# Linear attention after an AMM convolution block: heads re-sorted over row groups, two products of eight tiles for four of four, fewer matmuls in the averages, new ranks

## The chip, the cores and the metric

The kernel runs on one core of one Trainium2 chip. The metric is the device time of one execution in microseconds, lower is better. Engines are named as in the profile: PE (TensorE matmul), PEld (TensorE weight load), DVE (VectorE), ACT (ScalarE), POOL (GpSimd), SP (SyncE, which issues the DMAs).

## The reference

The input is x of 32 images, 1024 channels, 14 x 14 positions, float32. Layer 0 (table look-up convolutions with softmax weights, three of them, with batch norms) ends in a residual sum. Layer 1 is what the change is about; cut to what matters:

```python
x = gn(x)                                   # 32 groups of channels per image
q = elu(qk_w[:c] @ x[:, :half] + b) + 1     # 1024 channels out of 512
k = elu(qk_w[c:] @ x[:, half:] + b) + 1
q_rope, k_rope = rope(q), rope(k)           # pairs of channels turned by an angle of the position
# 16 heads of 64 channels, n = 196 positions
z   = 1 / (einsum('bhdn,bhd->bhn', q, k.mean(-1)) + 1e-6)
kv  = einsum('bhdn,bhen->bhde', k_rope, x) / n
out = einsum('bhdn,bhde->bhne', q_rope, kv) * z
x = x + out + depthwise_3x3(x) + lepe_b     # "lepe": nine taps per channel
```

The last einsum, `q_rope` times `kv`, is the query product.

## The kernel before

Layer 0 is written as three stages one after the other and fills the span to about 2277 us. Layer 1 follows under one instruction plan for 16 pairs of images (NP = 16).

**The plan.** `Plan.do(engine, rank, weight, fn, reads, writes, port, lag)` records a piece: a few instructions on one engine, with a rank (its due time) and a weight (an assumed duration). `Plan.write()` plays the pieces through: an engine that is free takes the ready piece of lowest rank whose buffers are free. The order so found is the order of each engine's instructions; on the chip they run in that order and wait on semaphores. `due` holds the ranks within a pair, `T` the step of ranks from pair to pair. Buffers are `Slot`s out of rings; PSUM has eight banks, in three rings: `mm` (4), `pa` (3) and `w` (1).

**One pair.** Channels lie in eight blocks of 128 partitions; `xts[h]` holds four of them (h = 0 or 1).
- `front` (8 pieces per pair): ACT scales a block into a `w` bank (L1639), DVE adds the third convolution's output (L1648), applies the ReLU and the residual (L1653) and takes statistics (L1658).
- `group_norm` (twice): PE averages the statistics over the 32 partitions of a group with the matrix `gavg`; two halves of each image are two matmuls that accumulate (L1695), once for the means and once for the variances, with small DVE steps between (L1703 to L1711).
- `channels` (16): the projection to q or k, 128 output channels by 392 positions, four matmuls (L1786), then two ACT pieces (L1795, L1798) and one on DVE (L1802). The even channels of a rope pair lie in r = 0, the odd ones in r = 1, so a q tile holds four heads, 32 partitions each, in two halves r.
- `rope` (8): four POOL instructions per tile. `v_tokens`, `k_tokens` (16): PE transposes, copied out by ACT (L1848, L1851). `products` (4): kv of four heads, eight or more small matmuls each in 32-column tiles (L1885).
- `normalisers`: DVE writes the means of k into `kmm` (L1918, two pieces), PE multiplies (L1936), DVE adds 1e-6 (L1945) and takes the reciprocal (L1946); the result goes through DRAM and back as a broadcast, and POOL multiplies it into the q tile (L1972).
- `attend` (4 pieces, one per q tile j): 16 matmuls in the code, 32 in the profile, since each float32 matmul shows as two (L1992). Head h of the tile contracts over partitions 32h to 32h+31 and writes 64 output channels: the tile on the array has 32 rows and 64 columns. Heads 0 and 1 write the two halves of one `pa` bank, heads 2 and 3 those of another, so the four tiles of a piece take each row group once.
- `lepe` (8): the eight side taps are added by DVE onto the `pa` bank (L2010), but one tap of each of blocks 4 to 7, which ACT and POOL do (`side_tap`, L2039 and L2047); then DVE adds the bank to x (L2024), which frees it. The middle tap is folded into the residual by ACT (L1752).
- The last pair has no successor to overlap with; there six of its eight blocks have their taps done on PE with diagonal matrices (`diagonal_taps`, L2066) before the query product accumulates onto them.

**Inputs.** Small tables and the first pair's x are loaded by SP during the third convolution: that stage calls one entry of the list `early` at the start of each of its 13 groups. The projection weights take the place of the convolution's tables, so `projection` issues their eight loads (L230) when layer 1 begins.

Of the kernel before, what the change touches and what calls it, by code (L numbers as in the profile page):

```python
# [17 lines left out]
P = 128  # L18
C = 1024
# [130 lines left out]
def conv_preact_kernel(ctx: ExitStack, tc: tile.TileContext, a: dict, out: bass.AP):  # L150
# [274 lines left out]

    def attention_inputs(stack):
# [3 lines left out]
        def loads(_):  # L430
# [6 lines left out]
            for n, k in (("qb", a["qb"]), ("kb", a["kb"].rearrange("o (r j p) -> p (o r) j", p=P, r=2))):  # L437
                nc.sync.dma_start(tile_(n, [P, 2, 4]), k)
                tile_(n + "u", [P, 2, 4])
                tile_(n + "d", [P, 2, 4])  # L440
# [3 lines left out]
            for n in ("cosq", "sinq"):  # L444
                t = tile_(n, [P, 4, 14])
                v = a[n].rearrange("p j (r c) -> p j r c", c=14)
                nc.sync.dma_start(t[:, :2], v[:, :2, :, 0])
                nc.sync.dma_start(t[:, 2:], v[:, 2:, 0, :])
# [12 lines left out]
            for h in (1, 0):  # L461
                for i in range(2):
                    nc.sync.dma_start(
                        given[f"x{h}"][:, :, i * HW : (i + 1) * HW],
                        x[i, 4 * h * P : 4 * (h + 1) * P].rearrange("(c q) n -> q c n", q=P),
                    )

# [28 lines left out]
        def projection(b):  # L496
            t = a["wkT" if b < 4 else "wqT"]
            return lambda: load_lut(b, t[(b % 4) * P : (b % 4 + 1) * P])

        return [loads, third, tables, heads], [projection(b) for b in range(8)], [third]  # L500
# [990 lines left out]
    with ExitStack() as s:  # L1491
# [57 lines left out]
        T = 80.0  # L1549
# [22 lines left out]
        for n, k in (("mm", 4), ("pa", 3), ("w", 1)):  # L1572
# [8 lines left out]
        for n, shape in (  # L1581
# [3 lines left out]
            ("gq", [P, 8, 2]),  # L1585
            ("gve", [P, 8]),
# [41 lines left out]
        def front(p, h, c, xt, ot, rank):  # L1628

            ch = 4 * h + c  # L1630
            w = Slot("pa" if p == 0 and c % 2 else "w")
# [49 lines left out]
        def group_norm(p, h, rank):  # L1681
# [10 lines left out]
            def average(ps, src):  # L1692
                def piece():
                    for k in range(2):
                        nc.tensor.matmul(  # L1695
                            ps()[:, :8], gavg, src[:, :, k], start=(k == 0), stop=(k == 1)
                        )

                return piece

            def centred():
# [5 lines left out]
                )  # L1707
                nc.vector.tensor_scalar(g("nmc"), pm()[:, :8], -1.0, None, ALU.mult)
# [18 lines left out]
            do(PE, rank, 0.42, average(pm, mean), gst, [pm], lag=0.3)  # L1727
            do(DVE, rank, 0.55, centred, [pm, *gst], [key("gq"), key("nmc")])
            do(PE, rank, 0.42, average(pv, g("gq")), [key("gq")], [pv], lag=0.3)
# [45 lines left out]
        def channels(p, keys, j, r, t, sums, rank):  # L1775
# [7 lines left out]
            def product():  # L1783
                m0 = r * 512 + j * P
# [87 lines left out]
        def products(i, jp, kts, vts, rank):  # L1872
# [4 lines left out]
            def piece():  # L1877
                pv = pk()[:, :256].rearrange("p (j r e) -> p j r e", j=2, r=2)
                for j in range(2):
                    for r in range(2):  # L1880
                        for h in range(2):
                            for q in range(4):
                                c0 = (2 * (2 * jp + j)) * P + 64 * q
# [29 lines left out]
        def normalisers(p, qs, ks, rank):  # L1913


            def means(i):
                def piece():
                    nc.vector.tensor_tensor(  # L1918
# [9 lines left out]
            for i in range(2):  # L1928
                do(DVE, rank - 10, 0.2, means(i), allk, [("kmm", i)], port=True)
# [14 lines left out]
            def inverse():  # L1944
                nc.vector.tensor_scalar(z, pd()[:, :HW], 1e-6, None, ALU.add)  # L1945
                nc.vector.reciprocal(z, z)  # L1946
# [6 lines left out]
            do(DVE, rank - 10, 1.7, inverse, [pd], ["z"])  # L1953
# [27 lines left out]
        def attend(j, kvs, qr, pa, rank, onto):  # L1981

            def piece():
                for i in range(2):
                    for r in range(2):
                        for h in range(4):
                            v = slice(32 * h, 32 * h + 32)
                            n = 210 - 14 * i  # L1990
                            e = slice(64 * (h % 2), 64 * (h % 2) + 64)
                            nc.tensor.matmul(  # L1992
                                pa[h // 2]()[e, i * 210 : i * 210 + n],
                                kvs[i, j // 2]()[v, j % 2, r],
                                qr()[v, r, i * HW : i * HW + n],
                                start=(r == 0 and not onto),
                                stop=(r == 1 and (i == 1 or not onto)),
                            )

            do(PE, rank, 1.65, piece, [kvs[0, j // 2], kvs[1, j // 2], qr], pa, lag=0.25)  # L2000
# [76 lines left out]
        def store(p, h, xt, rank):  # L2077
# [14 lines left out]
        unread = once.tile([P, HW], F32, tag="unread", name="unread")  # L2092


        due = dict(
            front_k=-64,
            front_q=-30,
            channel=9.0,
            norm=19,
            normalised=33,  # L2100
            middle=43,
            key=7.75,
            rope_k=-1.5,
            query=23,
            step=7.25,
            row=4.25,
            rope_q=74,
            v0=27,
            v_half=1.75,
            v1=69,  # L2110
            k0=41,
            k_half=3.0,
            k1=64,
            kv0=65,
            kv1=55,
            den=45,
            scaled=70,
            attend=75.5,
            sums=24,
            lepe=98,  # L2120
            taps=9.0,
            half=16.0,
            tap=2.75,
            side=99,
            diagonal=160,
        )

        def pair(p, t):
# [46 lines left out]
            js = (2, 3, 0, 1)  # L2175
            for n, j in enumerate(js):
                normalise_q(p, n, j, qrs[j], at["scaled"])
            last = p == NP - 1
            pools = {0: "pa pa", 1: "mm mm", 2: "pa w", 3: "mm mm"} if last else {}
# [99 lines left out]
```

## Time and profile before

| | |
|---|---|
| median of 3 runs | 3359.23 us (3357.97 to 3359.8) |
| profiled execution, its own time | 3358.99 us |
| its span | 3357.2 us |
| first projection of layer 1 (PE L1786) | at 2295.4 us |
| last query product (PE L1992) | at 3348.6 us |
| PE / DVE / POOL / ACT busy over the span | 98% / 85% / 75% / 53% |
| granted PE clock of the core | 0.994 |

A "busy" PE is not a PE at its peak: matmuls overlap. Here PE is read by the start of one piece to the start of the next, and an engine's load by the busy time within a stretch of whole pairs.

### The profile page before, as it was taken

How to read it: one execution, taken by the hardware profiler on the slowest of the kernel's cores; microseconds unless marked ns; L12 is line 12 of the kernel's file. 1: busy time of each engine (PE TensorE's matmuls, PEld its weight loads, DVE VectorE, ACT ScalarE, POOL GpSimd, SP SyncE). 2: the span in 40 equal slices, each digit the busy share in tenths (PEclk: the TensorE clock that was granted, in tenths of full speed). 3: DMA queues.
4: the chain of work that ended last, by engine and by line, in shares of the span. 5: the costliest groups of instructions: out<-in, count | busy, mean ns of one | idle time of the engine just before them, and what ended most of it. 6: DMA issues, size and time to landing. Idle time of an engine off the chain costs nothing. (4 is left out here: it accounts for less than half of the span.)

```text
span 3357.2 us, 61041 instructions
## 1 busy us (share of the span) xinstructions
PE 3296.6 (98%) x22297; PEld 2014.2 (60%) x22297; DVE 2864.6 (85%) x4174; ACT 1787.8 (53%) x4419; POOL 2534.2 (75%) x1558
## 2 busy tenths in 40 slices
PE   8999999999999999999999999998999999999999
PEld 4555555554454544444478888885666666666665
DVE  8999999997888899888656666755899999999996
ACT  5555555554444444444311111107888888888886
POOL 6999999997788889888432222215988888888888
PEclk9999999999999999999999999999999999999999
DMA  4110111103444344433231111113223333232321
GB/s 120 47 49 28 46 47 35 39 28 86 135 124 123 112 122 125 122 113 109 64 81 50 50 50 50 39 47 125 70 84 99 90 89 98 79 92 82 94 81 49
DMA packets 242251, 266.31 MB, mean 79 GB/s; under 512 B 32812, under 2 KB 239700, under 8 KB 241944
## 3 DMA queue, kind: packets, MB, share of 16 engines
q1 hardware_dynamic: 241248, 262.02, 26.3%
q8 instruction: 179, 2.93, 0.4%
q14 instruction: 128, 1.05, 0.1%
q10 hardware_dynamic: 696, 0.31, 0.0%
HBM read 171.01 MB, written 75.58 MB: 73 GB/s over the span
## 5 line engine op out<-in xcount | busy, mean ns | idle before, releaser
L622 POOL TENSOR_TENSOR t<-t,r 128x1568 f32<-128x1568 f32 (+3 forms) x288 | 961.8, 3340 | 519.7 <-issue 221.2
L742 PE MATMUL po<-t,lut 128*128 128x392 f32 x3840 | 1331.2, 499 | 4.9 <-DMA t<-spare 3.9
L742 PEld LDWEIGHTS po<-t,lut 128*128 128x128 f32 x3840 | 710.1, 190 | 604.2 <-issue 79.4
L1786 PE MATMUL mm<-y,lut 128*128 128x392 f32 x2048 | 714.5, 494 | 1.4 <-DVE k L1802 1.4
L584 DVE STREAM_TRANSPOSE tt<-t 128x1568 f32<-128x1568 f32 (+1 forms) x284 | 517.4, 1822 | 153.9 <-ACT t L572 149.6
L572 ACT ACTIVATE t<-sc,cbias 128x392 f32<-128x392 f32 (+1 forms) x624 | 322.5, 598 | 558.5 <-PE sc L905 187.7
L2010 DVE SCALAR_TENSOR_TENSOR pa<-y,lepe_w,pa 128x406 f32<-128x406 f32 x900 | 535.7, 636 | 19.1 <-PE pa L1992 16.8
L615 DVE STREAM_TRANSPOSE r<-rc 128x1568 f32<-128x1568 f32 (+1 forms) x284 | 520.8, 1834 | 11.6 <-POOL t L622 1.2
L1786 PEld LDWEIGHTS mm<-y,lut 128*128 128x128 f32 x2048 | 369.4, 188 | 242.9 <-issue 6.3
L587 POOL TENSOR_TENSOR tt<-tt 128x784 f32<-128x784 f32 x256 | 471.0, 1840 | 30.3 <-DVE tt L584 30.3
L572 ACT ACTIVATE t<-sc,room 128x392 f32<-128x392 f32 x512 | 259.1, 589 | 392.7 <-issue 163.8
L1368 PE MATMUL po<-t,lut 128*128 128x224 f32 (+2 forms) x1352 | 313.3, 414 | 0.0
L603 DVE TENSOR_REDUCE sm<-tt 128x98 f32<-128x784 f32 (+1 forms) x284 | 293.6, 1034 | 1.1 <-POOL tt L587 0.8
L1368 PEld LDWEIGHTS po<-t,lut 128*128 128x128 f32 (+1 forms) x1352 | 233.4, 189 | 62.9 <-issue 60.6
L605 DVE RECIPROCAL rc<-sm 128x98 f32<-128x98 f32 (+1 forms) x284 | 220.1, 775 | 9.8
L626 ACT ACTIVATE sm<-sm 128x98 f32<-128x98 f32 (+1 forms) x284 | 85.4, 301 | 153.8 <-DVE rc L605 153.8
L1972 POOL TENSOR_TENSOR qr<-qr,zb 128x784 f32<-128x784 f32 x64 | 118.3, 1856 | 46.0 <-DMA zb<-zd 45.7
L1639 ACT ACTIVATE w<-x,tb,gn_a 128x196 f32<-128x196 f32 x248 | 128.3, 517 | 35.3 <-POOL y L1521 28.2
L1798 ACT ACTIVATE e<-e 128x392 f32<-128x392 f32 x256 | 134.4, 525 | 1.0
L1035 PE MATMUL sc<-patch,room 27*32 27x392 f32 x4096 | 122.9, 507 | 8.9 <-DMA patch<-h1d 8.9
L1381 DVE TENSOR_TENSOR o<-po,o 128x224 f32<-128x224 f32 (+1 forms) x156 | 81.5, 543 | 56.8 <-PE po L1368 51.9
L1752 ACT ACTIVATE y<-x,gb,ga 128x196 f32<-128x196 f32 x256 | 123.3, 541 | 12.1 <-POOL gb L1715 12.1
(215 smaller groups left out, 4517.9 us busy)
## 6 DMA issues: line engine op xcount, KB each, us to landing
patch<-h1d SPq DMA_DIRECT2D x383, 108.5 KB
x<-in_x_dram SPq DMA_DIRECT2D x32, 784.0 KB
o3d<-o SPq DMA_DIRECT2D x56, 448.0 KB
x<-in_x_dram SPq DMA_DIRECT2D x64, 392.0 KB
out_dram<-x SPq DMA_DIRECT2D x64, 392.0 KB
o<-o3d SPq DMA_DIRECT2D x62, 392.0 KB
h1d<-pad SPq DMA_DIRECT2D x96, 225.0 KB
patch<-h1d SPq DMA_DIRECT2D x383, 54.2 KB
```

The costliest lines, as they stand in the source:

```text
L572: nc.scalar.activation(t[:, j, : sc.shape[1]], sc, AF.Identity if exact else AF.Exp, bias=bias[:, j : j + 1],)
L584: nc.vector.transpose(tt, tf)
L587: nc.gpsimd.tensor_tensor(tv[:, :, :8], tv[:, :, :8], tv[:, :, 8:], ALU.add)
L603: nc.vector.tensor_reduce(sm, tv, AX.X, ALU.add)
L605: nc.vector.reciprocal(rc, sm)
L615: nc.vector.transpose(r, bc(rc, 2, KC))
L622: nc.gpsimd.tensor_tensor(v[:, c], v[:, c], r[:, c], ALU.mult)
L742: nc.tensor.matmul(po[h], luts[b][:, j, h * P : (h + 1) * P], ts[u % len(ts)][:, j, :N2], start=(b == 0 and j == j0), stop=(b == 7 and j = ...
L1368: nc.tensor.matmul(dst, w, x, start=start, stop=stop)
L1786: nc.tensor.matmul(pv(), w[kt][:, m0 : m0 + P], ywin(p, first + kt), start=(kt == 0), stop=(kt == 3),)
L1798: nc.scalar.activation(e(), e(), AF.Exp, scale=-1.0)
L2010: nc.vector.scalar_tensor_tensor(acc, neighbours(p, c, offset(k)), lw[:, c, k : k + 1], acc, ALU.mult, ALU.add,)
```

## The change

1. **Heads.** The projections' output channels are re-sorted, so that q tiles 2jp and 2jp+1 hold the heads (0, 3, 4, 7) and (1, 2, 5, 6) of the half jp, 32 partitions each. Row group q of the two tiles then holds the two heads of channel block c = q, one per column half. `attend` does both tiles in one piece: 32 matmuls in the code, in the order that goes over all eight 32 x 64 tiles, into four `pa` banks at once. There are two such pieces per pair, each with weight `ATT` = 2.0 where four had 1.65.
2. **Loads for it.** The weights are loaded by three DMAs of 32- and 64-element runs for each of the eight row blocks, in place of one DMA of whole rows; the biases and the angle tables, by 16 DMAs each, in four further entries of `early`.
3. **Averages.** DVE adds the two halves (`halves`, twice per `group_norm`), and each average is one matmul.
4. **Normalisers.** The two pieces for `kmm` go from DVE to POOL; adding 1e-6 goes from DVE to ACT, with the constant in a new tile `tiny`.
5. **Banks.** `mm` 4 and `pa` 4; `front` takes its bank from `mm`.
6. **Side taps** for blocks 0, 3, 4 and 7 in place of 4 to 7; in the last pair the first half's banks are `pa`, the second half's `mm`.
7. **Ranks.** All of `due`, and `T`.

```diff
+    HEADS_OF = (0, 3, 4, 7), (1, 2, 5, 6)
+    heads_in = lambda t: slice(1, 3) if t else slice(0, 4, 3)
...
+        def bias(n, k):
+            def piece(_):
+                for j in range(4):
+                    for o in range(2):
+                        for r in range(2):
+                            src = k[:, r, j // 2 * 2 + o].rearrange("(h d) -> h d", d=32)
+                            dst = given[n][64 * o : 64 * o + 64, r, j : j + 1]
+                            nc.sync.dma_start(dst, src[heads_in(j % 2)])
...
+        def angles(n):
+            def piece(_):
+                v = a[n].rearrange("(h d) j (r c) -> h d j r c", c=14, d=32)
+                for j in range(4):
+                    for q in range(4):
+                        o, h = divmod(HEADS_OF[j % 2][q], 4)
...
+                        nc.sync.dma_start(given[n][32 * q : 32 * q + 32, j], src)
...
-            return lambda: load_lut(b, t[(b % 4) * P : (b % 4 + 1) * P])
...
+            def load():
+                v = w[:, 32:480].rearrange("p (n m) -> p n m", m=64)
+                src = t[:, 64:960].rearrange("p (n m) -> p n m", m=P)
+                nc.sync.dma_start(v, src[:, :, 32:96])
+                nc.sync.dma_start(ends(w, 512), ends(t, C))
+                v = w[:, 512:].rearrange("p (n m) -> p n m", m=64)
+                nc.sync.dma_start(v, t.rearrange("p (n m) -> p n m", m=P)[:, :, 32:96])
...
-        return [loads, third, tables, heads], [projection(b) for b in range(8)], [third]
+        return [loads, qb, kb, angles("cosq"), angles("sinq"), third, tables, heads], [projection(b) for b in range(8)], [third]
...
-        T = 80.0
+        T = 81.22
+        SIDES = [0, 3, 4, 7]
+        ATT = 2.0
...
-        for n, k in (("mm", 4), ("pa", 3), ("w", 1)):
+        for n, k in (("mm", 4), ("pa", 4)):
...
-            w = Slot("pa" if p == 0 and c % 2 else "w")
+            w = Slot("pa" if p == 0 and c % 2 else "mm")
...
-                    for k in range(2):
-                        nc.tensor.matmul(
-                            ps()[:, :8], gavg, src[:, :, k], start=(k == 0), stop=(k == 1)
-                        )
...
+            def average(ps):
+                return lambda: nc.tensor.matmul(ps()[:, :8], gavg, g("gs"), start=True, stop=True)
+
+            def halves(src):
+                nc.vector.tensor_reduce(g("gs"), src, AX.X, ALU.add)
...
-            do(PE, rank, 0.42, average(pm, mean), gst, [pm], lag=0.3)
-            do(DVE, rank, 0.55, centred, [pm, *gst], [key("gq"), key("nmc")])
-            do(PE, rank, 0.42, average(pv, g("gq")), [key("gq")], [pv], lag=0.3)
+            do(DVE, rank, 0.1, lambda: halves(mean), gst, [key("gs")])
+            do(PE, rank, 0.21, average(pm), [key("gs")], [pm], lag=0.3)
+            do(DVE, rank, 0.65, centred, [pm, *gst], [key("gs"), key("nmc")])
+            do(PE, rank, 0.21, average(pv), [key("gs")], [pv], lag=0.3)
...
-                m0 = r * 512 + j * P
+                m0 = j % 2 * 512 + (2 * r + j // 2) * P
...
-                                c0 = (2 * (2 * jp + j)) * P + 64 * q
+                                c0 = 512 * jp + 64 * HEADS_OF[j][q]
...
-                    nc.vector.tensor_tensor(
+                    nc.gpsimd.tensor_tensor(
                         kmm[i].rearrange("p r j h -> p (r j) h")[:, :, i:8:2],
...
-                do(DVE, rank - 10, 0.2, means(i), allk, [("kmm", i)], port=True)
+                do(POOL, rank - 10, 0.3, means(i), allk, [("kmm", i)], port=True)
...
-                nc.vector.tensor_scalar(z, pd()[:, :HW], 1e-6, None, ALU.add)
-                nc.vector.reciprocal(z, z)
+            def more():
+                nc.scalar.activation(z, pd()[:, :HW], AF.Identity, bias=tiny)
...
-            do(DVE, rank - 10, 1.7, inverse, [pd], ["z"])
+            do(ACT, rank - 10, 0.3, more, [pd], ["z"])
+            do(DVE, rank - 10, 1.3, lambda: nc.vector.reciprocal(z, z), [], ["z"])
...
-        def attend(j, kvs, qr, pa, rank, onto):
+        def attend(jp, kvs, qrs, pas, rank, onto):
...
                     for r in range(2):
-                        for h in range(4):
-                            v = slice(32 * h, 32 * h + 32)
...
+                        for q in range(4):
+                            v = slice(32 * q, 32 * q + 32)
+                            for j in range(2):
+                                c, h = divmod(HEADS_OF[j][q], 2)
+                                nc.tensor.matmul(
+                                    pas[c]()[64 * h : 64 * h + 64, i * 210 : i * 210 + n],
+                                    kvs[i, jp]()[v, j, r],
+                                    qrs[j]()[v, r, i * HW : i * HW + n],
...
-            do(PE, rank, 1.65, piece, [kvs[0, j // 2], kvs[1, j // 2], qr], pa, lag=0.25)
+            do(PE, rank, ATT, piece, [kvs[0, jp], kvs[1, jp], *qrs], pas, lag=0.25)
...
-            front_k=-64,
-            front_q=-30,
-            channel=9.0,
...
-            attend=75.5,
-            sums=24,
-            lepe=98,
+            front_k=-58.62,
+            front_q=-30.11,
+            channel=17.14,
...
+            attend=93.22,
+            sums=8.99,
+            lepe=102.05,
...
-            pools = {0: "pa pa", 1: "mm mm", 2: "pa w", 3: "mm mm"} if last else {}
-            for n, j in enumerate(js):
-                pa = [Slot(b) for b in pools.get(n, "pa pa").split()]
-                by_pe = last and n < 3
+            for m, jp in enumerate((1, 0)):
+                pools = ["mm"] * 4 if last and m else ["pa"] * 4
+                pas = [Slot(b) for b in pools]
                 taps = {}
...
+                by_pe = [last and 2 * m + k // 2 < 3 for k in range(4)]
...
-                    for m in range(3 if last else c // 4):
+                    for _ in range(3 if last else c in SIDES):
...
+                attend(jp, kvs, qj, pas, at["attend"] + due["sums"] * 2 * m, by_pe)
```

## The prediction

> **What bounds the kernel now.** I read the busy times by stage first. Only layer 1 (2277 us to the end) is touched beyond a few loads, and it is periodic, so I took the chain of work that ended last and looked for the same step in successive pairs:
>
> ```profile
> 2932.58 2.64 PE mm L1786 x8
> 2997.00 2.64 PE mm L1786 x8
> 3061.72 2.68 PE mm L1786 x8
> 3126.17 2.71 PE mm L1786 x8
> 3190.80 2.64 PE mm L1786 x8
> ```
>
> The columns are start, length and step. A pair takes (3190.80 - 2932.58) / 4 = 64.55 us, and the chain stays almost wholly on PE. The busy times of just these four pairs (the columns are PE, PEld, DVE, ACT, POOL, then clock, DMA share and GB/s):
>
> ```profile
> 2932.60:3190.80 258.20, 256.18 (x2497) 166.63 (x2497) 248.41 (x528) 220.03 (x545) 228.52 (x208) 1.00 0.31 90
> ```
>
> Divided by four, PE has work in 64.05 of 64.55 us, DVE 62.1, POOL 57.1, ACT 55.0. PE sets the pace, but DVE has only 2.45 us per pair to spare. So whatever PE saves beyond that is worth nothing unless DVE is relieved too. The waits of DVE in these four pairs say what the 2.45 us consist of:
>
> ```profile
> DVE pa L2010 <- PE pa L1992: 3.5, 2, 1.9
> DVE q L1802 <- ACT e L1798: 1.8, 3, 0.9
> DVE w L1648 <- ACT w L1639: 1.5, 3, 0.8
> ```
>
> In total, number, longest: few and short. The costs of the PE pieces come from the timeline (start, length, then x instructions); the length of a piece includes the tail of its last matmul, so I take start to next start:
>
> ```profile
> 868.18 0.94 PE L1035 MATMUL sc<-patch,room 27*32 27x392 f32 x32
> 869.63 5.50 PE L742 MATMUL po<-t,lut 128*128 128x392 f32 x16 [0.51 <-DMA t<-spare]
> ...
> 2923.83 1.99 PE L1885 MATMUL mm<-vt,kt 105*32 105x64 f32 x128
> 2925.75 0.68 PE L1848 MATMUL mm<-ident,kr 128*105 128x128 f32 x4
> ...
> 2946.28 0.51 PE L1695 MATMUL mm<-gq,gavg 128*128 128x8 f32 x4
> 2946.72 1.60 PE L1992 MATMUL pa<-qr,kv 32*64 32x210 f32 x32
> 2948.25 2.90 PE L1786 MATMUL mm<-y,lut 128*128 128x392 f32 x8
> ```
>
> A query product takes 2948.25 - 2946.72 = 1.53 us for 32 matmuls, 48 ns each; an average 0.44 us (others 0.36 to 0.43).
>
> **Query products, per pair.** Now 4 x 1.53 = 6.1 us. A full-array matmul of 392 columns takes 2.64 / 8 = 0.33 us, so one of 203 (the mean of 210 and 196) streams for 0.17 us; 32 of them four at a time are 8 x 0.17 = 1.37 us, and the measured 1.53 is that and a start-up. So four tiles do run at once. Eight at a time would take 64 / 8 x 0.17 + 0.16 = 1.53 us for two q tiles: the lower bound. The upper one is no more overlap than now, 3.06 us. That more than four tiles overlap, columns of one row group included, is in the L1035 row: 32 matmuls of 392 columns in 32 x 32 tiles last 0.94 us in all, where eight in a row take 2.64. I take 1.9 us: the change books 2.0 in the plan, and the plan's weights stand 0.11 to 0.13 above the trace (1.65 for 1.53; 1.6 for the 1.47 of L1936; 1.15 for the 1.04 of 64 matmuls of L1885). Saved: 6.1 - 3.8 = 2.3 us (0 to 3.1). The piece after a product is late by 0.1 (2.74 for 2.64 us in L1786); two fewer of these, 0.2.
>
> The issue rate could stand in the way: 64 matmuls in 1.9 us are 30 ns each. L1885 shows 128 with their weight loads in 2925.75 - 2923.83 = 1.92 us, 15 ns each, so the row leaves room. The Trainium skill ("TensorE: Matmul & The Clock Gate", section "Wait — 56ns, not 53.3ns?") says that matmuls never start less than about 25 ns apart; by that floor the product would take 1.6 us, and the L1885 row is below the floor.
>
> **Averages.** Four pieces of about 0.41 us lose half of their matmuls: 4 x 0.2 = 0.8 us saved on PE. DVE gains four small reductions of 0.16 us (the nearest rows, L1708 and L1711, are 8 columns wide and last 0.156 and 0.158): +0.64 us (0.3 to 0.9, as they follow a dependent step or not). The second one lies between gq and the PE average, on the chain of the group norm, whose successor (POOL's power, then ACT's normalisation) has tens of microseconds of rank ahead of the projections: no cost but DVE's time.
>
> **Normalisers.** DVE loses two pieces of 0.39 us (L1918) and one of 0.35 (L1945): -1.13 us. POOL gains two of 128x32, between its own 0.2 us for 128x8 and DVE's 0.39: +0.6, to 57.7. ACT gains one of 196 columns, 0.36 as in L1806: to 55.4. Neither becomes the bound. What queues behind them are POOL's rope steps and ACT's exponentials; the ranks are ten before the due time, so that the wait for the reciprocal is not the last one.
>
> **Sum per pair.** PE 64.55 - 2.3 - 0.2 - 0.8 = 61.25; DVE 62.1 + 0.64 - 1.13 = 61.6. So DVE becomes the pace, by a hair, with PE next. Before, PE as the single bound lost 0.5 us of 64.55; two engines this near to each other lose more. If DVE keeps none of its 2.45 us of waiting the pair takes 61.6, if it keeps all 64.05. I take a third, the share that is hand-over from ACT (the lines L1798 and L1648 above and smaller ones, about 0.9 us per pair): 62.4 us. Gain 2.15 us per pair, for 15 steps from pair to pair 32 us.
>
> **Banks.** A product now needs all four `pa` banks empty, so DVE has no taps to do from its last sum onto x until the product is done; it has to fill some 2 to 5 us (1.9 for the product, and up to 2.64 for the projection that PE is in) from its 25 us per pair that are not taps or sums (62.1 less 60 x 0.55 and 8 x 0.47). That is cover enough if such work is ready; I price it at nothing here and as a rival below. `front` now shares `mm`: eight holdings of some 2.5 us beside 16 of about 5 for the projections and smaller ones, by my count under 60% of four banks.
>
> **The start.** Layer 1's first projection begins at 2295.4 and needs all four key weights. They were issued at 2277.7, behind two 392 KB loads:
>
> ```profile
> 2277.71 1.88 SPq L230 DMA_DIRECT2D lut<-in_wkT_dram  x4
> 2279.63 3.15 SPq L230 DMA_DIRECT2D lut<-in_wqT_dram  x4
> ...
> 2295.44 21.32 PE L1786 MATMUL mm<-y,lut 128*128 128x392 f32 x64
> ```
>
> At the 361 GB/s of that stretch 0.8 + 2.1 MB are there by about 2286. Now four weights are 4 x 128 x 17 = 8704 runs of 128 or 256 B. The old angle tables give the price of a short run: between 1703.2 and 1709.4 us there were
>
> ```profile
> DMA packets 8107, 0.26 MB, mean 42 GB/s; under 512 B 7891, under 2 KB 8107, under 8 KB 8107
> ```
>
> 8107 packets in 6.2 us on 16 engines, 12.2 ns each. 8704 such are 6.6 us, with the bytes' own 5.8 us on top 12.5: landing by 2293, just in time. The far bound is the mean packet of the stretch from 2277.5 (5163 packets in some 22.3 us on 16 engines: 69 ns, mostly bytes), which would make it 38 us and the start 24 us late. I take +1, the short-run row being the nearest in size. SP issues 24 DMAs for 8, at 0.47 to 0.79 us 8 to 13 us more; the loads behind them (x of pair 1, read by ACT at 2312) have 12 us or more to spare. The Trainium skill ("DMA: Bandwidth & Descriptors", section "Specifications") puts the least transfer for full rate at 512 B, which speaks against these runs; it gives no time for them.
>
> The 64 small loads of `early` go out 16 to a group, 0.43 to 0.7 us each: 7 to 11 us of SP, in a gap that SP has in each group (it issues at 1744.1 to 1746.0 and next at 1763.9): hidden. Without the gap they would delay the t<-t transfers by as much, four times.
>
> **The tail.** The last pair's final product now holds all four blocks of the first half, two of which have five DVE taps each to come; before, those two were attended at 3328.4 and their taps ran under PE's work. After the product stand 10 x 0.55 + 4 x 0.48 = 7.4 us in place of 1.0; PE gets there earlier by its savings, some 2.3: +4 us (0 to +7).
>
> **Sum.** 3359.0 (the profiled execution; the median is 3359.2) - 32 + 1 + 4 = 3332 us.
>
> **The rivals.**
> - *As summed* (0.66). From 61.6 and no loss at the ends to 63.2 us per pair and 10 us lost there: 3315 to 3349.
> - *DVE stands at the four banks* (0.17), slower. For it: DVE's longest wait is the one for L1992 already, with two or three banks; and there is no spare engine left. Against: four pairs hold just 3.5 us of it. Each product of 62.4-us pairs may cost 0.9 us more stall before the gain is gone (64.55 - 0.3 for the ends - 62.4 = 1.85 for two). At 1.5 us each the pair takes 65.4: 3359 + 15 x 0.85 + 5 = 3377.
> - *Eight tiles do not overlap* (0.08): the change does not do what it says. Two tiles of a row group would stream one after the other. PE then saves 1.0 per pair: 3359 - 15 + 5 = 3349. The L1035 row speaks against it.
> - *The weights come late* (0.09), by half of the far bound: 3332 + 12 = 3344.
>
> About 0.2% (7 us) is what a measurement of this kernel can tell from no change. Faster by more than that: 0.63 of the first case, 0.06 and 0.08 of the last two, 0.77 in all; slower 0.17, nearly all from the banks; within it 0.06. The range 3314 to 3368 takes in the first, third and fourth cases and the mild part of the second. The first case's own range is 3315 to 3349.
>
> **What would show it.** Right: the step of the chain falls to 62 to 63 us; L1992 shows two pieces of 64 per pair, 1.5 to 2.0 us each; DVE busy near 61.6 per pair and 98% or more, PE just below; the first L1786 within 2 us of 2295.4. Wrong: L1992 at 3 us; DVE waiting for L1992 over 2 us per product; the first projection after 2300; ACT or POOL as the releaser of most of DVE's idle time.

## The result, and the profile after

The changed kernel takes 3338.47 us (median of 4 runs, 3336.69 to 3344.3) against 3359.52 for the kernel before in the same measurement: ratio 0.994, 95% interval 0.9923 to 0.9957. The prediction was 3332, in the range 3314 to 3368. The profiled execution took 3338.64 us, its span is 3336.5.

Inside layer 1 the two profiled executions part like this (before, after; from the starts of the instructions):

| | before | after | difference |
|---|---|---|---|
| first load of the stage to first projection | 18.8 us | 29.2 | +10.4 |
| first projection to the start of the last one | 1013.9 | 981.0 | -32.9 |
| start of the last projection to the end | 47.8 | 49.3 | +1.5 |
| first load of the stage to the end | 1080.5 | 1059.5 | -21.0 |

So the steady part gave the 32 us of the sum, the tail cost less than the 4, and the start, priced at 1, took 10 back.

In the changed kernel the lines have other numbers: L1826 is the projection, L2031 the query product, L1734 the average, L2049 the side taps, L1842 DVE's step of q and k, L1888 the transposes, L1680, L1689 and L1694 the front pieces on ACT and DVE, L1792 the normalisation.

The chain of work that ended last (start, length, step), at the step that recurs in each pair:

```profile
2703.93 18.71 PE mm L1826 x56
2765.93 18.71 PE mm L1826 x56
2827.92 18.72 PE mm L1826 x56
```

A steady pair is now 62.0 us, each like the last but for one of 62.2 in the four shown next; before, they varied round 64.6. The busy times of four pairs (PE, PEld, DVE, ACT, POOL, then clock, DMA share, GB/s):

```profile
2703.90:2952.20 248.30, 241.94 (x2465) 156.02 (x2465) 243.62 (x533) 220.18 (x549) 230.86 (x217) 1.00 0.33 94
```

By four: of 62.08 us DVE is busy 60.9 (98.1%), PE 60.5, POOL 57.7, ACT 55.0. PE and DVE have changed places, and DVE is now the pace. What DVE still waits for in those pairs, every wait that the view lists:

```profile
DVE gd L1741 <- PE mm L1734: 2.5, 4, 0.6
DVE q L1842 <- ACT e L1838: 1.0, 4, 0.3
DVE k L1842 <- POOL ru L1871: 0.2, 1, 0.2
```

The query product (L2031) is not in the list: holding four banks at once costs DVE no wait here. The largest term is the average of the group norm, for which DVE now stands in every pair. In the four pairs of before it had stood for it once:

```profile
DVE gd L1703 <- PE mm L1695: 0.3, 1, 0.3
```

The timeline of PE round the first product of a pair (start, length, instructions last):

```profile
2722.56 1.63 PE L2031 MATMUL pa<-qr,kv 32*64 32x210 f32 x64
2724.12 0.39 PE L1734 MATMUL mm<-gs,gavg 128*128 128x8 f32 x2
2724.36 2.02 PE L1888 MATMUL mm<-ident,kr 128*105 128x128 f32 x16
```

64 matmuls take 2724.12 - 2722.56 = 1.56 us, where two q tiles took 3.06. That is the lower bound of the prediction (1.53), not the 1.9 it chose. An average, one matmul that shows as two, takes 2724.36 - 2724.12 = 0.24 us here (0.14 to 0.24 in this pair).

The start, on SP (timeline of the DMA queue), from the first load of the stage over the first and the last of the 24 weight loads to pair 1's x:

```profile
2276.97 1.02 SPq L1659 DMA_DIRECT2D qr<-o3d  x2
2278.04 0.46 SPq L531 DMA_DIRECT2D lut<-in_wkT_dram  x1
...
2294.17 0.55 SPq L534 DMA_DIRECT2D lut<-in_wqT_dram  x1
2294.76 1.22 SPq L1644 DMA_DIRECT2D x<-in_x_dram  x2
```

and on ACT, with the idle time before each line and what ended it in brackets:

```profile
2299.11 0.52 ACT L1680 ACTIVATE mm<-x,tb,gn_a 128x196 f32<-128x196 f32 x1 [13.20 <-DMA x<-in_x_dram]
...
2303.41 0.52 ACT L1680 ACTIVATE mm<-x,tb,gn_a 128x196 f32<-128x196 f32 x1 [1.83 <-DMA x<-in_x_dram]
2304.60 0.52 ACT L1680 ACTIVATE mm<-x,tb,gn_a 128x196 f32<-128x196 f32 x1 [0.67 <-DMA x<-in_x_dram]
2305.05 3.62 ACT L1792 ACTIVATE y<-x,gb,ga 128x196 f32<-128x196 f32 x8
```

SP issues weights for 16.7 us (5.1 before), so x of pair 1 leaves at 2294.8 instead of 2283.9. In ACT's new order the front pieces of pair 1 (L1680) stand ahead of pair 0's normalisation (L1792), whose operands POOL had ready at 2294.3. The first projection starts at 2306.1, one microsecond after the start of that normalisation.

The chain of work that ended last does not go by ACT here, but by DVE. SP issues another load behind the weights, pair 1's part of the third convolution (`o`); DVE's front pieces of pair 1 (L1689) stand 8.05 us for it. Behind them in DVE's order come the steps of pair 0's second averages (L1741), and PE has the last of these averages ahead of the first projection. DVE's timeline, then the chain:

```profile
2292.92 0.17 DVE L1737 TENSOR_REDUCE gs<-gst 128x8 f32<-128x16 f32 x1
2301.14 0.63 DVE L1689 SCALAR_TENSOR_TENSOR mm<-o,sc,mm 128x392 f32<-128x392 f32 x1 [8.05 <-DMA o<-o3d]
...
2304.49 0.16 DVE L1741 TENSOR_TENSOR gd<-gst,mm 128x16 f32<-128x16 f32 x1
```

```profile
2305.51 0.57 PE mm L1734 x2
...
2306.13 15.80 PE mm L1826 x40
```

So two paths reach the first projection at nearly the same time, one over x and ACT, one over `o` and DVE. Both begin with a load behind the weights, and in both work of pair 1 stands ahead of pair 0's.

### The profile page after: what moved, and what is told of

Its sections match the earlier page's. It is cut to its first block, busy times and chain, and to the rows that moved or that the text cites. A ratio compares the mean times of both kernels' runs of the same rounds, so it can differ in the third digit from the quotient of the medians.

```text
span 3336.5 us, 60995 instructions
## 1 busy us (share of the span) xinstructions
PE 3242.5 (97%) x22169; PEld 1974.6 (59%) x22169; DVE 2841.2 (85%) x4191; ACT 1787.1 (54%) x4435; POOL 2538.4 (76%) x1590
## 5 line engine op out<-in xcount | busy, mean ns | idle before, releaser
L1826 PE MATMUL mm<-y,lut 128*128 128x392 f32 x2048 | 706.9, 496 | 4.6 <-DVE k L1842 3.5
L1826 PEld LDWEIGHTS mm<-y,lut 128*128 128x128 f32 x2048 | 375.6, 188 | 268.3 <-DVE k L1842 10.6
L653 DVE STREAM_TRANSPOSE r<-rc 128x1568 f32<-128x1568 f32 (+1 forms) x284 | 520.8, 1834 | 11.6 <-POOL t L660 1.2
L2049 DVE SCALAR_TENSOR_TENSOR pa<-y,lepe_w,pa 128x406 f32<-128x406 f32 x900 | 527.7, 635 | 2.1 <-PE pa L2031 1.9
L1406 PEld LDWEIGHTS po<-t,lut 128*128 128x128 f32 (+1 forms) x1352 | 233.4, 189 | 62.9 <-issue 60.2
L1680 ACT ACTIVATE mm<-x,tb,gn_a 128x196 f32<-128x196 f32 x248 | 126.9, 516 | 48.8 <-POOL y L1559 28.4
L854 ACT ACTIVATE x<-x,gn_b,gn_a 128x196 f32<-128x196 f32 x256 | 127.6, 559 | 0.0
```

The costliest lines, as they stand in the source:

```text
L653: nc.vector.transpose(r, bc(rc, 2, KC))
L1406: nc.tensor.matmul(dst, w, x, start=start, stop=stop)
L1680: nc.scalar.activation(wv()[:, image(i)], xc()[:, image(i)], AF.Identity, bias=tb[:, ch, b : b + 1], scale=gn_a[:, ch, b : b + 1],)
L1826: nc.tensor.matmul(pv(), w[kt][:, m0 : m0 + P], ywin(p, first + kt), start=(kt == 0), stop=(kt == 3),)
L2049: nc.vector.scalar_tensor_tensor(acc, neighbours(p, c, offset(k)), lw[:, c, k : k + 1], acc, ALU.mult, ALU.add,)
```

## The experiments

All kernels fix the order in which `Plan.write` goes through the engines, by one line in place of `engines = {p[0] for p in self.pieces}`; why is told under the tenth. With the order used, the instructions of the changed kernel are those of its profile on every engine. "Pair" is a quarter of the window of four pairs as above. The first load of layer 1 comes between 2275.7 and 2282.4 us in the profiled executions, though nothing before it was edited; so the last column, from there to the end, compares them more closely than the time does. The changed kernel was not measured again beside the experiments; the kernel before was (experiment 10: 3360.36 for 3359.52), and q_after_x, whose steady pairs are the same, lies within 1 us of it.

| kernel | time, us | pair | DVE / PE busy per pair | first load to first projection | first load to end |
|---|---|---|---|---|---|
| changed | 3338.47 | 62.08 | 60.9 / 60.5 | 29.2 | 1059.5 |
| four_tiles | 3355.58 | 62.91 | 61.1 / 61.7 | 29.8 | 1074.7 |
| q_after_x | 3339.24 | 62.06 | 60.9 / 60.5 | 30.5 | 1059.7 |
| x_then_q | 3333.89 | 62.06 | 60.9 / 60.5 | 22.7 | 1055.3 |
| dve_plus | 3378.28 | 64.88 | 62.9 / 62.0 | 29.4 | 1099.1 |
| pe_plus | 3357.13 | 63.16 | 61.0 / 61.9 | 30.1 | 1077.4 |
| old_average | 3349.89 | 62.33 | 60.4 / 61.0 | 29.6 | 1065.0 |
| norm_on_dve | 3353.26 | 63.05 | 62.0 / 60.8 | 30.1 | 1074.8 |
| best_try | 3347.43 | 63.01 | 60.8 / 60.7 | 23.4 | 1069.3 |

**1. Four tiles at a time** (`attend`).

```diff
-                for i in range(2):
+                for j in range(2):
+                    for i in range(2):
...
-                            for j in range(2):
```

> The 64 matmuls of a query product are issued q tile by q tile (j outermost), so that four 32x64 tiles are in use at a time and not eight; nothing else differs, the order on the other engines included. Theory (eight tiles overlap, and PE's relief is what let DVE set the pace): a product takes 3.0 to 3.1 us instead of 1.56, PE 63.5 of a pair instead of 60.5, the pair 64.2 to 64.6 instead of 62.07, the time 3338 + 15 x 2.3 = 3370 to 3376. Rival (the new ranks and DVE's relief brought the gain, PE's product little of it): the pair 62 to 62.8, the time below 3350.

The timeline of PE, and a line of DVE's waits over four pairs:

```profile
2726.85 2.39 PE L2031 MATMUL pa<-qr,kv 32*64 32x210 f32 x64
2729.17 0.39 PE L1734 MATMUL mm<-gs,gavg 128*128 128x8 f32 x2
```

```profile
DVE pa L2049 <- PE pa L2031: 2.7, 8, 0.5
```

The product takes 2.32 us, not 3.0. The records of the single matmuls say why: each q tile's rounds of four come about 0.18 us apart, but where the first tile ends and the second begins the rounds of both lie between each other, 0.03 to 0.14 us apart. The tiles of the second q tile are free and do not wait for the first to finish. So this undoes half of the overlap (0.76 of 1.50 us), and the pair grows by 0.83: 0.7 of it is new waiting of DVE for this product. Both expected ranges were missed, the theory's for that reason; the direction is the theory's. With an unchanged order on every other engine, the eight tiles are worth at least 13 us of the 33 (0.83 us in 15 pairs), since half of the overlap was left.

**2. VectorE's extra work** (in `variance`).

```diff
+                [nc.vector.tensor_scalar(spent, tb.rearrange("p c b -> p (c b)"), 1.0, None, ALU.add) for _ in range(2)]
...
```

> VectorE gets four more operations of 128x256 per pair, whose result nobody reads. Between the rows of 128x8 (0.159 us) and 128x392 (0.555) one should last 0.2 to 0.42 us, so 0.8 to 1.7 us per pair. Theory (DVE sets the pace, busy 60.9 of 62.07): the pair grows by all of it, 12 to 25 us in the time, 3350 to 3363. Rival (PE sets the pace and DVE has its 1.1 us to give): the pair grows by at most 0.6 us, the time to 3347 at most.

The busy times of four pairs, and two of DVE's waits in them (the line numbers of the average are one lower here):

```profile
2784.17:3043.69 259.52, 247.91 (x2464) 160.23 (x2465) 251.51 (x549) 222.22 (x549) 231.49 (x217) 0.97 0.32 90
```

```profile
DVE gd L1740 <- PE mm L1733: 4.2, 4, 1.1
DVE k L1842 <- ACT e L1838: 1.0, 4, 0.2
```

DVE is busy 1.97 us more per pair (an operation lasts 0.47, above the bracket I gave), and the pair grows by 2.80: all of it and 0.8 more. DVE sets the pace; the rival is out, though the time overshoots the theory's range too. Most of the 0.8 is in the waits: 0.4 us per pair more for PE's average (4.2 us in four pairs for 2.5) and 0.25 for ACT's exponentials (1.0, of which the changed kernel lists none). The granted clock is 0.97 where the changed kernel has 1.00; whether that lengthened the waits is open.

**3. TensorE's extra work** (`average`).

```diff
-                return lambda: nc.tensor.matmul(ps()[:, :8], gavg, g("gs"), start=True, stop=True)
+                return lambda: [nc.tensor.matmul(ps()[:, :8], gavg, g("gs"), start=True, stop=True) for _ in range(3)]
```

> TensorE does each matmul of the averages three times (the same result), 8 more per pair at 0.2 us: 1.6 us, PE 62.1 instead of 60.5. Theory (DVE sets the pace, PE has 1.5 us to give): most of it is hidden until PE comes level with DVE; the pair grows by 0.4 to 0.9 us, the time to 3344 to 3352. Rival (PE sets the pace): the pair grows by all of 1.6 us, the time to 3362.

The waits of DVE for the average in four pairs:

```profile
DVE gd L1741 <- PE mm L1734: 5.2, 4, 1.3
DVE gve L1750 <- PE mm L1734: 1.6, 4, 0.4
```

The pair grows by 1.08, between the two theories. The waits for the average were 2.5 us in four pairs and are 6.8: 1.08 per pair, the whole growth, at the same DVE busy time. PE's busy time grew by 1.36 us. So it is not PE's sum that binds: PE's pieces that DVE stands waiting for count for most of their length, while PE itself, at 61.9 of 63.16, still has room.

**4. Query weights after the first half of x**: the closures of `weights4[4:]` are kept in a list `held` and run in `third` of pair 1.

```diff
+                    while p and held: held.pop(0)()
...
-            do(SP, b - 90, 0.95, weights4[b], (), [("w", b)], lag=3.5 + b)
+            do(SP, b - 90, 0.95, weights4[b] if b < 4 else lambda b=b: held.append(weights4[b]), (), [("w", b)], lag=3.5 + b)
```

> The twelve loads of the four query weights are issued by SP after pair 1's first loads of x and of the third convolution instead of before them; the order on the four other engines is the same. Theory (the late x of pair 1, on which ACT stands, puts the first projection late): x is issued near 2287 instead of 2294.8, ACT's first piece of pair 1 starts by 2293, the first projection falls from 2306 to 2297 to 2299, the time by 7 to 9 us, to 3330. Rival (the key weights, in their short runs, are themselves what is late): the first projection stays within 2 us of 2306 and the time within 2 us of 3338.

ACT, as in the last fence of the result:

```profile
2296.26 0.52 ACT L1680 ACTIVATE mm<-x,tb,gn_a 128x196 f32<-128x196 f32 x1 [5.79 <-DMA x<-in_x_dram]
...
2309.33 0.52 ACT L1680 ACTIVATE mm<-x,tb,gn_a 128x196 f32<-128x196 f32 x1 [10.44 <-DMA x<-in_x_dram]
...
2310.97 3.62 ACT L1792 ACTIVATE y<-x,gb,ga 128x196 f32<-128x196 f32 x8
```

A miss for the theory as I had put it: nothing was gained. ACT's first piece of pair 1 came 14.7 us after the first load instead of 22.1, but the second half of x was still behind the query weights (SP issued it 22.7 us after the first load, 20.1 in the changed kernel), and ACT stood there instead.

**5. Query weights after both halves of x**: as 4, but `held` is emptied behind pair 1's second load of x (`while not h and held: held.pop(0)()` in `quad`).

> As q_after_x, but the query weights' loads are issued after both of pair 1's halves of x and after their parts of the third convolution; the order on the four other engines is the same as in the changed kernel. In q_after_x ACT stood 10.4 us at the second half of pair 1's x, which its query weights had pushed back, so the first projection came 30.5 us after the first load of the stage (29.2 in the changed kernel, 18.8 in the kernel before). Theory (ACT stands on both halves of pair 1's x before it normalises pair 0): 20 to 23 us after the first load, the time 6 to 9 us less than 3338.5. Rival (the key weights' short runs are late themselves): still 28 us or more.

ACT again:

```profile
2292.65 0.52 ACT L1680 ACTIVATE mm<-x,tb,gn_a 128x196 f32<-128x196 f32 x1 [6.17 <-DMA x<-in_x_dram]
...
2297.11 0.52 ACT L1680 ACTIVATE mm<-x,tb,gn_a 128x196 f32<-128x196 f32 x1 [1.80 <-DMA x<-in_x_dram]
...
2298.66 3.62 ACT L1792 ACTIVATE y<-x,gb,ga 128x196 f32<-128x196 f32 x8
```

The first projection now comes 22.7 us after the first load, 6.5 earlier, with the same order on the four other engines. What was late were the loads of pair 1 behind the weights, x for which ACT stands and `o` for which DVE stands; the edit moves both, and no run tells their shares apart. The key weights were in time for this. 4.2 us of the 6.5 reach the end, less than the 6 to 9 expected: PE now waits 3.4 us for DVE's first pieces of pair 1 (L1694), which hold `mm` banks (PE's waits from 2285 to 2345 us):

```profile
PE mm L1826 <- DVE x L1694: 3.4, 2, 3.2
```

At 3333.89 us (3331.36 to 3336.1) this kernel is the fastest of all runs, ahead of the changed one by 4.6 us; the two were measured in different sessions, and their ranges lie 0.6 us apart.

**6. The averages as before.**

```diff
-                return lambda: nc.tensor.matmul(ps()[:, :8], gavg, g("gs"), start=True, stop=True)
+                return lambda: [nc.tensor.matmul(ps()[:, :8], gavg, src[:, :, k], start=k == 0, stop=k == 1) for k in range(2)]
...
-                nc.vector.tensor_reduce(g("gs"), src, AX.X, ALU.add)
+                return
...
```

> The averages are again two accumulating matmuls on TensorE, and VectorE does no half sums; the order on the engines is the same. PE gains 4 x 0.2 = 0.8 us per pair, DVE loses 4 x 0.17 = 0.68. Theory (DVE sets the pace; an average counts only as long as DVE waits for it, and the half sum before it is on the same path): the pair stays at 62.07 or falls by up to 0.7, the time 3328 to 3341. Rival (the prediction's step, in which the relief of PE is worth having): the pair grows by 0.2 to 0.5, the time 3341 to 3346.

The pair grows by 0.25 us in the window, 0.3 as a mean over all fifteen steps (985.6 for 981.0 us): in the rival's range for the pair, and against the theory. Of the time, 5.4 of the 11.4 us lie ahead of the first load of layer 1 in the profiled execution, where nothing was edited, so that time overstates it; first load to end says +5.5. (Where the other three runs lose theirs is not on record.) DVE is busy 0.54 us less, but waits longer for the average; its waits in four pairs:

```profile
DVE gd L1741 <- PE mm L1734: 4.6, 4, 1.2
DVE q L1842 <- ACT e L1838: 1.9, 4, 0.5
DVE gve L1750 <- PE mm L1734: 0.8, 4, 0.2
```

Waits for the average go from 2.5 to 5.4 us in four pairs, 0.72 per pair, and the 0.54 of half sums are paid back with a loss. The half sums are worth it because they shorten a wait of the pacing engine; PE, at 61.0 of 62.33, has room in either case.

**7. The normalisers on VectorE again.**

```diff
-                    nc.gpsimd.tensor_tensor(
+                    nc.vector.tensor_tensor(
...
-                nc.scalar.activation(z, pd()[:, :HW], AF.Identity, bias=tiny)
+                nc.vector.tensor_scalar(z, pd()[:, :HW], 1e-6, None, ALU.add)
```

> The means of the keys and the addition of 1e-6 are done by VectorE again and not by GpSimd and ScalarE: DVE gains 1.13 us per pair by the rows of before, 62.0 instead of 60.9. Theory (DVE sets the pace; in dve_plus 1.96 us more of DVE's work made the pair 2.8 us longer): the pair grows by 1.1 to 1.6, the time 3355 to 3363. Rival (PE or the plan's due times set the pace): by less than 0.5, the time below 3346.

The busy times of four pairs:

```profile
2836.51:3088.70 252.19, 243.04 (x2465) 156.45 (x2465) 247.97 (x545) 219.48 (x545) 229.55 (x209) 1.00 0.34 92
```

DVE 62.0 instead of 60.9, as priced, and the pair 0.97 longer at 98.3% of DVE: microsecond for microsecond, a little under the theory's range and far over the rival's.

**8. The normalisers alone, on the kernel before** (the same two edits the other way round, and the `tiny` tile).

> One part of the change done alone on the kernel before (its order pinned as in before_pinned, and the same on every engine): the means of the keys on GpSimd, the addition of 1e-6 on ScalarE. DVE loses 1.13 us per pair, PE nothing. Theory (before the change PE sets the pace, busy 64.05 of 64.55 us, so DVE's relief alone is worth next to nothing): the pair shortens by 0 to 0.2, the time 3357 to 3361. Rival (DVE sets the pace already before, and the new layout of the heads is worth little): the pair shortens by 0.8 to 1.1, 3343 to 3348.

The busy times in the window that the prediction showed for the kernel before, and a line of DVE's waits in it:

```profile
2932.60:3190.80 258.20, 255.64 (x2495) 166.53 (x2494) 244.51 (x515) 220.13 (x548) 228.73 (x215) 1.00 0.31 90
```

```profile
DVE z L1946 <- ACT z L1945: 2.6, 4, 1.2
```

DVE is busy 61.1 us per pair in place of 62.1 and the time is 3360.47, as for before_pinned (3360.36). The microsecond turns into waiting, 0.65 of it for the step that went to ACT, because PE still has 63.9 of 64.55. The same edit is worth 1.0 us per pair after the change and nothing before. (It is not quite the same: here DVE's reciprocal follows ACT's addition within one piece, so DVE stands for it; in the changed kernel they are two pieces.)

**9. The old ranks in the changed kernel.**

```diff
-        T = 81.22
+        T = 80.0
```

and all of `due` as before.

> The changed kernel with the table of due times and the T of the kernel before. Theory (the sums of DVE's and PE's work set the time, the ranks only the waits between them): DVE keeps its 60.9 us per pair and some more waiting, the pair 62.3 to 64, the time 3342 to 3365; the first projection comes earlier than 29 us after the first load, since pair 1's front pieces are ranked behind pair 0's normalisation again. Rival (the ranks are what brought the gain): the pair is back at 64.5 or more, the time 3355 to 3375.

The waits between 2500 and 3000 us, some seven pairs (total, number, longest):

```profile
POOL qr L2012 <- DMA zb<-zd: 45.0, 16, 6.1
ACT mm L1680 <- DMA x<-in_x_dram: 27.0, 10, 6.6
DVE mm L1689 <- ACT mm L1680: 26.3, 8, 6.4
```

3417.95 us, slower than either kernel: first to last projection takes 1067.1 us, 86 more than in the changed kernel. Worse than both theories had it. The sums of DVE and PE are the floor only under an order that fits; this one lets ACT stand for x, and DVE for ACT. The start is 17.8 us, a microsecond under that of before the change, though SP issues the same 24 weight loads first and pair 1's x leaves only at 2295.7: ACT normalises pair 0 without standing for it. That is the half of the cause that lies in the ranks. So the new ranks are a condition of the gain and one of the two conditions of the late start. What they would give the kernel before by themselves was not run; PE, busy there in 64.05 of 64.55 us, left them half a microsecond per pair at most if its work stays as it is; that is argued from its busy time, not shown.

**10. The order of ties.** `Plan.write` goes through a Python set of engine names; its order differs between builds, and with it which engine takes a piece first at equal times.

```diff
-        engines = {p[0] for p in self.pieces}
+        engines = ["PE", "DVE", "ACT", "POOL", "SP"]
```

> The kernel before, with one line changed: the planner goes through the engines in a fixed order instead of in that of a Python set, so that every build gives the order of instructions that the profiled kernel before had. Theory (the kernel before takes 3359 us in the first runs and 3379 us beside the experiments because ties in the plan are broken by the order of a set, which differs from build to build): 3357 to 3362 us here, with the unpinned kernel before at 3379 beside it. Rival (these runs are on another chip or in another state): both near 3379.

3360.36 us, against 3379.93 for the unpinned kernel before in the same runs. So the 20 us between the two groups of times of the kernel before are not the chip's. That the slower group had the other order is inferred; its trace was not taken. For that reason times here are compared with 3338.47 and 3359.52, not with the kernel before run beside the experiments.

**11. The other tie order in the changed kernel** (ACT ahead of PE and DVE in the list).

> The changed kernel with the planner going through the engines in another fixed order (ScalarE before TensorE and VectorE), which gives the second of the two orders of instructions that ties can lead to. Nothing else differs. Theory (DVE's and PE's sums set the pair, and in the steady pairs both orders leave DVE little waiting): the pair 62 to 62.5, the time 3338 to 3350. Rival (a tie decides as much as in the kernel before, where it is worth 20 us): the pair 63 or more, the time 3352 or more.

3352.26, at the rival's bound and 13.8 us more than the changed kernel; in the profiled execution 11.3 from the first load. Most steady pairs are 62.0 here too, some 63 to 64.5. Two thirds of what the whole change brings hangs on a tie.

**12. Two more small steps off VectorE**, on top of 5.

```diff
-                nc.vector.tensor_scalar(g("nmc"), pm()[:, :8], -1.0, None, ALU.mult)
+                nc.scalar.activation(g("nmc"), pm()[:, :8], AF.Identity, scale=-1.0)
...
-                nc.vector.tensor_scalar(g("gve"), pv()[:, :8], EPS, None, ALU.add)
+                nc.scalar.activation(g("gve"), pv()[:, :8], AF.Identity, bias=eps)
...
```

> x_then_q, and two small steps of the group norm (the negated mean and the addition of its epsilon, 0.155 us each, four per pair) go from VectorE to ScalarE, where they read the same banks. Theory (DVE sets the pace): DVE 60.9 - 0.62 = 60.3 us per pair and 0.2 less waiting for the second average; the pair 61.2 to 61.6, the time 3334 - 15 x 0.6 = 3325 (3321 to 3330). Rival (PE, with 60.5, or ScalarE's new waits for the averages take over): the pair stays at 61.8 to 62.4, the time 3331 to 3340.

Some waits of four pairs:

```profile
ACT nmc L1747 <- PE mm L1888: 7.6, 4, 1.9
PE mm L1888 <- ACT vt L1891: 5.7, 9, 0.9
DVE gd L1741 <- PE mm L1734: 3.8, 4, 0.9
DVE k L1842 <- ACT e L1838: 2.3, 4, 0.6
```

Wrong on both counts: the pair is 0.95 longer than in x_then_q. DVE's busy time fell by 0.1 us per pair and not by 0.62, since these short steps overlap their neighbours (in the timeline of the changed kernel L1747 lasts 0.16, and the next instruction starts 0.07 after it). ACT now stands 1.9 us per pair ahead of the negated mean, the copies behind it come late, PE waits for those (5.7 us for 1.1 in the changed kernel), and DVE for PE and ACT.

## Why the prediction was right, and where it was not

- **Sign, pace and query product.** Eight tiles overlap, PE's busy time falls from 64.05 to 60.5, DVE becomes the pace at 98%. (The forecast of 61.25 was counted down from the pair's 64.55; from the busy time the same savings give 60.75.) The product's 1.9 us were over-sized: it measures 1.56, 0.34 less twice per pair. The reason for choosing 1.9, the plan's own weight less a usual margin, was weaker than the streaming bound computed beside it.
- **DVE.** 61.6 forecast, 60.9 measured. norm_on_dve confirms the 1.13 for the normalisers (1.09), old_average puts the half sums at 0.54, where 0.64 was taken; some 0.6 us less come with the new order, and no run separates the cause. The traces show only where it lies: added up row by row, DVE's durations fall from 71.8 to 71.4 us per pair (71.1 in x_then_q), near the 0.5 that was priced; the rest is that neighbouring rows overlap more, and a busy time counts an overlap once. "A third of the waiting stays" gave 0.8 us of idle time per pair; it is 1.2, and other waits than the hand-overs named: 0.6 of it is the average.
- **The averages.** The step said "no cost but DVE's time" for the half sum and booked 0.8 on PE. Both were the wrong column: the average lies on DVE's path (pe_plus, old_average), and halving its matmuls is worth 0.3 us per pair there. ("Others 0.36 to 0.43" was also read too narrowly; some took 0.46 and 0.47.)
- **Gain per pair.** 2.15 forecast; 2.5 in steady pairs. Over all fifteen steps the first to last projection gave 32.9, against 32, since the first and last pairs gave less.
- **The start, the term that failed.** +1 forecast, +10.4 measured. The weights' bytes and SP's extra 8 to 13 us (it is 11.6) were priced, but "the loads behind them (x of pair 1, read by ACT at 2312) have 12 us or more to spare" took the 2312 from the order of before. The new ranks put that reading ahead of pair 0's normalisation, and DVE's reading of `o` ahead of pair 0's second averages, and the slack was gone. x_then_q takes back 6.5 us by moving x and `o`, and old_ranks 11.4 by the old order. The rival that names weights coming late had about the price and the wrong thing that is late. "The first projection after 2300" was one of the prediction's own signs of being wrong, and it came true (2306.1); its signs of being right in the steady pairs came true as well.
- **The tail.** +4 forecast, +1.5 measured: 13.8 us follow the start of the last product where 8.6 did, and PE gets there 3.7 us sooner.
- **The four banks.** The rival is out: DVE has no wait for L2031 in the four pairs.
- **Early small loads.** Hidden as priced: the four groups take SP 9.1 to 10.4 us each, and its next transfer still starts at 1763.93 (1763.90 before).

Against the sum the start is 9.4 us worse, the tail 2.5 and the steady stretch 0.9 better, so the time lies 6.5 us above the 3332. The mechanism of the steady pairs was right; that the stretch came out within 1 us of its 32 is luck, for there the product and DVE's sum were better than priced, DVE's waits and the first and last pairs worse. And the range, 54 us wide, had room for the term that failed.

## What to carry to other kernels

Price a step by the engine that will set the pace afterwards: the same microsecond of VectorE was worth nothing before this change and a whole one after it, and a piece of another engine counts as long as the pacing engine stands waiting for it. When ranks or due times change with the work, do not take slack from the old order: look for in-order queues in which something that waits for a late load now stands ahead of the first work. Where a list scheduler breaks ties by the order of a set, fix the order before comparing anything; here it moved the changed kernel's time by 14 us and, by inference, that of the kernel before by 20.

## What the runs showed of the hardware

- Matmuls in small tiles start far closer than one streaming time. In the records of L2031 the eight of a round start 6 to 7 ns after one another, and rounds follow every 0.17 to 0.18 us (the first after 0.23), which is the 0.17 us that one matmul of 203 columns streams. The Trainium skill ("TensorE: Matmul & The Clock Gate", section "Wait — 56ns, not 53.3ns?") has a floor of about 25 ns between starts. The mean here, 1.56 us / 64 = 24.4 ns, would fit it, but the single starts do not; what bounds the product is each tile's own streaming.
- A tile that is free starts while others still stream, across the seam of two unrelated groups (four_tiles: 2.32 us instead of two times 1.5).
- While the weights went in runs of 128 and 256 B, other loads beside them, 268 and 265 GB/s were moved at DMA shares of 1.12 and 1.26 (2278 to 2286 and 2286 to 2294 us); before, with whole rows, 348 and 392 at 0.98 and 1.05.
- The granted clock was lower in the two kernels whose PE idled most in the stretches shown: 0.97 in dve_plus (PE busy 95.5%) and 0.96 in old_ranks (90.3%), against 1.00 in the changed kernel (97.4%) and in norm_on_dve (96.4%). What sets it, no run here separates.
